# A recommender forward pass on one core: counts and sums 27 steps ahead of the token rows for 16, the last blocks of layers queued, five outputs of the last tile begun early, zero rows by transfer

## The chip, the cores and the metric

The kernel runs on one core of a Trainium2 chip. A core has TensorE (PE: matrix products, with a separate record, PEld, for its weight loads), VectorE (DVE), ScalarE (ACT), GpSimd (POOL) and SyncE (SP), and sixteen DMA engines which move data between HBM and the on-chip memory. Each engine works through its own instructions in the order of the program; semaphores make one wait for another. The metric is the device time in microseconds of one launch, as the median of several runs.

## The reference

For each of 16384 examples, 32 token ids pick rows of 300 numbers from a table of 50000 rows, and their mean is taken. Three fields of 20 ids each pick rows of 64 numbers from tables of 1000, 5000 and 10000 rows, and the mean is taken in each. Four single ids pick rows of 64 from tables of 100, 50, 20 and 1000 rows. The eight parts are joined to 748 numbers and go through three dense layers of 1024, 512 and 256 outputs. Beside this, every id of the seven small tables has one scalar ("wide"), and all of them are added to the last product.

```python
tok = word_emb[token_idx].mean(axis=1)              # 32 rows of 300
e1 = emb_mh1[mh1_idx].mean(axis=1)                  # 20 rows of 64; e2, e3 alike
...
o1 = emb_oh1[oh1_idx]                               # one row of 64; o2, o3, o4 alike
emb = jnp.concatenate([tok, e1, e2, e3, o1, o2, o3, o4], axis=1)
wide = (wide_mh1[mh1_idx].sum(axis=(1, 2)) + ... + wide_oh4[oh4_idx][:, 0])[:, None]
h = jax.nn.relu(emb @ W1 + b1)
h = jax.nn.relu(h @ W2 + b2)
h = jax.nn.relu(h @ W3 + b3)
return jax.nn.sigmoid(h @ Wd + bd + wide)
```

All of it is float32.

## The kernel before

**Tiles.** The examples are cut into 128 tiles of 128. Three things are done for each tile.

*Token rows.* POOL gathers the rows by indirect DMA: one DMA takes one token position of the 128 examples (L279). Two positions share a buffer `tok_rows` of a pool with `TOK_BUFS` buffers, so a tile has 16 groups of two gathers. DVE adds a group to the running sum `own` in PSUM (L260 for the first group of a tile, L262 and L267 for each later one); the last addition of a tile writes into the tile's feature buffer `g`. The additions stand `TOK_LAG` = 3 groups behind the gathers in the program. There are 2048 groups, and with the lag `n_all` = 2051 units of work. The gather of a group waits until the buffer it takes was added up.

*Small tables.* They are never gathered. An id is split into a high part (which slice of 128 rows of the joined tables, 138 slices in all) and a low part (which row in it). DVE writes one-hot rows of both parts (L344), ACT scales half of one (L351), PE multiplies them for each pair of examples (L362), which gives the counts of every table row, and ACT evicts these to `cnt` (L365). Then PE multiplies the counts with the tables, slice by slice, 138 products a tile (L397), and DVE evicts the sums to `g` (L387). There is one PSUM buffer `pg` for these sums. The tables are held as three bfloat16 terms per number (`terms`), which are made at the start from raw rows (`load_tables`, `convert_tables`, L168 to L223). Where a table's length is not a multiple of 128, the rows that are missing are set to zero by DVE (L180).

*Layers.* When all features of a tile are there, PE transposes `g` in six chunks (L435) and DVE evicts them, scaled, to `x` (L439). Tiles are joined to blocks of `LAYER_TILES` = 3; the last two tiles, 126 and 127, are blocks of their own. I number blocks by their place for the threes (block 41 holds tiles 123 to 125) and by their tile for the two single ones (block 126, block 127). `mlp` (L509) is the work of a block: three layers (L493, evicted by ACT at L504), the last product `po` (L524), the addition of the wide term on DVE (L529), the sigmoid on ACT (L530) and the transfer of the result by SP (L532). The outputs of layers 1, 2 and 3 lie in turn in two buffers, "odd" and "even"; the third shares its buffer with the first, and the result row that SP sends out lies in it too.

**The order.** It is written out by hand in one loop over steps (L607). A tile's counts take `STEPS` = 11 steps, t is the tile whose counts are made and i the step in it; the sums of tile t − 1 run in the same 11 steps, in portions given by i. The loop has `n_steps` = 128 x 11 + `WAKE` steps. Token work is spread evenly over all of them (`toks.to(n_all * (step + 1) / n_steps)`, L650), so counts and sums drift ahead of the token rows from 0 steps at the start to `WAKE` at the end, and the last `WAKE` steps hold token rows and layers but no counts.

A tile that has its sums and its wide term is put on the list `waiting`; at a later step, when its tokens are added up, its transposes are emitted (L637 to L642). When a block has all its tiles, the layers of the block before are finished at once, whatever is left of them, and the new block's are begun (L643 to L649). Layers are generators that yield after every product, wrapped in `Paced`: each step takes as many products as brings the block to its share of the steps up to a limit, `left` (L649), which is where the tokens of the next block are complete (`ready`) and no later than `EARLY` = 3 steps before the end.

Evictions are kept on lists so that they come behind other work of the same step: `later` for DVE's (emitted by `flush`), `pending` for ACT's. At step `n_steps` − 3, `early_part` begins four of the eight outputs of layer 1 of the last tile, with the three chunks that need no tokens. Behind the loop come what is left of the layers, the other three transposes of tile 127, and its layers.

Of the kernel before, what the change touches and what calls it, by code (L numbers as in the profile page):

```python
# [8 lines left out]
F32 = mybir.dt.float32  # L9
# [5 lines left out]
AF = mybir.ActivationFunctionType  # L15
# [3 lines left out]
P = 128  # L19
N_TOK, TOK_D = 32, 300  # L20
N_MH, EMB = 20, 64
ROW = EMB + 1
D1, D2, D3 = 1024, 512, 256
TOK_GROUP = 2
TOK_LAG = 3
TOK_BUFS = 7
HOT_BUFS = 3
WAKE = 16
EARLY = 3
BLOCK = 256  # L30
LAYER_TILES = 3
LAST_TILES = 2
# [9 lines left out]
LAYER_TIME = 2.5  # L42
# [20 lines left out]
def kernel(  # L63
# [29 lines left out]
    for f in SMALL:  # L93
        n = -(-tables[f].shape[0] // P)
# [2 lines left out]

    tokp = ctx.enter_context(tc.tile_pool(name="tok", bufs=TOK_BUFS))
    const = ctx.enter_context(tc.tile_pool(name="const", bufs=1))
    idxp = ctx.enter_context(tc.tile_pool(name="idx", bufs=3))  # L100
    keyp = ctx.enter_context(tc.tile_pool(name="keys", bufs=1))
    scp = ctx.enter_context(tc.tile_pool(name="sc", bufs=2))
    ohp = ctx.enter_context(tc.tile_pool(name="onehot", bufs=HOT_BUFS))
    cp = ctx.enter_context(tc.tile_pool(name="counts", bufs=2))
    gp = ctx.enter_context(tc.tile_pool(name="g", bufs=2))
    wp = ctx.enter_context(tc.tile_pool(name="wide", bufs=2))
    xp = ctx.enter_context(tc.tile_pool(name="x", bufs=2))
    hp = ctx.enter_context(tc.tile_pool(name="h", bufs=1))
# [2 lines left out]
    ps_g = ctx.enter_context(tc.tile_pool(name="ps_g", bufs=1, space=bass.MemoryType.PSUM))  # L111
# [45 lines left out]
    first = const.tile([P, 2, N_SMALL], I32, name="first")  # L157
# [7 lines left out]
    minus_count = const.tile([P, P], BF16, name="minus_count")  # L165
    nc.vector.tensor_single_scalar(minus_count, ident, -1.0 / COUNT, op=ALU.mult)

    def load_tables(part0, tag):  # L168
        raw = hp.tile([P, PART, ROW], F32, name="raw", tag=tag)
        for f in SMALL:  # L170
            table, (h0, h1) = tables[f], slices[f]
            full, rest = divmod(table.shape[0], P)
            a, b = max(h0, part0), min(h0 + full, part0 + PART)
            if a < b:
                nc.sync.dma_start(
                    out=raw[:, a - part0 : b - part0, :],
                    in_=table[(a - h0) * P : (b - h0) * P, :].rearrange("(h p) d -> p h d", p=P),
                )
            if rest and part0 <= h0 + full < part0 + PART:
                nc.vector.memset(raw[:, h0 + full - part0, :], 0.0)  # L180
                nc.sync.dma_start(out=raw[0:rest, h0 + full - part0, :], in_=table[full * P :, :])
        return raw

# [229 lines left out]
    class Block:  # L413
# [2 lines left out]

        def __init__(self, first, n):
            self.first, self.n, self.missing = first, n * P, NK * n
            self.x = xp.tile([P, NK, N], F32, name="x")

        def transpose(self, t, ks):

# [34 lines left out]
    def early_part(block):  # L457


        part = []  # L460
        for pair in range(2):
            two = ps_c.tile([P, 2, 512], F32, name="pc")
            for m in range(2):
                part.append(two[:, m, :])
                for k in range(N_EARLY):
                    nc.tensor.matmul(
                        part[-1][:, 0 : block.n],
                        w1_sb[: chunk_k[k], k, (2 * pair + m) * P : (2 * pair + m + 1) * P],
                        block.chunk(k),
                        start=(k == 0),  # L470
                        stop=False,
                    )
        return part

    pending = []

    def flush_outputs():
        while pending:
# [2 lines left out]
    def layer(dst, weights, bias, srcs, n_out, part=None):  # L481


        n = srcs[0].shape[-1]
        for m in range(n_out):
            begun = part is not None and m < 4
            ph = part[m] if begun else ps_h.tile([P, N], F32, name="ph", tag="ph")
            for k, src in enumerate(srcs):
                if begun and k < N_EARLY:
                    continue  # L490
                if k == len(srcs) - 1:
                    flush_outputs()
                nc.tensor.matmul(  # L493
                    ph[:, 0:n],
                    weights[: src.shape[0], k, m * P : (m + 1) * P],
                    src,
                    start=(k == 0),
                    stop=(k == len(srcs) - 1),
                )
                if k < len(srcs) - 1:  # L500
                    yield 1

            def evict(m=m, ph=ph):
                nc.scalar.activation(dst[:, m, 0:n], ph[:, 0:n], AF.Relu, bias=bias[:, m : m + 1])  # L504

            pending.append(evict)
            yield 1

    def mlp(block, part=None):  # L509


        n = block.n
        h1 = hp.tile([P, M1, N], F32, name="h1", tag="odd")
        yield from layer(h1, w1_sb, b1_sb, [block.chunk(k) for k in range(NK)], M1, part)
        h2 = hp.tile([P, M2, N], F32, name="h2", tag="even")
        yield from layer(h2, w2_sb, b2_sb, [h1[:, k, 0:n] for k in range(M1)], M2)
        flush_outputs()
        h3 = hp.tile([P, M3 + 1, N], F32, name="h3", tag="odd")
        yield from layer(h3, w3_sb, b3_sb, [h2[:, k, 0:n] for k in range(M2)], M3)
        po = ps_h.tile([1, N], F32, name="po", tag="ph")  # L520
        for k in range(M3):
            if k == M3 - 1:
                flush_outputs()
# [4 lines left out]
        y = h3[0:1, M3, 0:n]  # L528
        nc.vector.tensor_add(y, po[:, 0:n], block.wide())  # L529
        nc.scalar.activation(y, y, AF.Sigmoid, bias=bd_sb)  # L530
        b0 = block.first * P
        nc.sync.dma_start(out=out[b0 : b0 + n, :].rearrange("n o -> o n"), in_=y)  # L532

    class Paced:

# [50 lines left out]
    def ready(t):  # L586

        return max(-(-(n_groups * (t + 1) + TOK_LAG) * n_steps // n_all) + 1, (t + 2) * STEPS + 2)

    def block_for(t):  # L590
        if t not in block_of:
            n = ends[t] - t
            block = Block(t, n)
            block_of.update({t + k: block for k in range(n)})
        return block_of[t]
# [7 lines left out]
    sc, evict = key_columns(lookup_keys(ix))  # L603
    evict()
    hot = one_hots(sc, 0, 0)
    layers, cnt, sums, waiting = None, None, None, []
    for step in range(n_steps):  # L607
        t, i = divmod(step, STEPS)
        s = t % NSUB
# [24 lines left out]
            flush_outputs()  # L634
        if sums:
            run_sums(sums, early_sums.get(i, 0), step, step)
        if waiting and step >= waiting[0][0]:  # L637
            _, k, ks = waiting[0]
            if k in summed or ks[0] < N_EARLY and k == tiles - 1:
                waiting.pop(0)  # L640
                block = block_for(k)
                later.append((step, block.transpose(k, ks)))  # L642
                if not block.missing:  # L643
                    flush(step)
                    if layers:
                        layers.finish()
                    layers = Paced(mlp(block), LAYER_TIME * block.n / P)
                    last = block.first + block.n // P
                    begin, left = step, min(ready(ends[last] - 1) if last < tiles else n_steps, n_steps - EARLY) - step  # L649
        toks.to(n_all * (step + 1) / n_steps)  # L650
        if t < tiles and more and s == 1 and i == 5:
            next_sc, evict = key_columns(next_keys)
# [2 lines left out]
        if sums:  # L655
            ahead = n_h * (i + 1) / STEPS - sums_done[i + 1]
        if layers:
            layers.to(mlp_work * layers.size * (step + 1 - begin) / left + ahead)
        if sums:
            run_sums(sums, late_sums.get(i, 0), step, step + 1)  # L660
        flush(step)
        if i == 0 and 2 <= t <= tiles + 1:
            wide_term(features(t - 2))
            if t - 2 < tiles - 1:
                waiting.append((step + 2, t - 2, range(NK)))
            else:
# [48 lines left out]
```

## Time and profile before

| | |
|---|---|
| time, median of 3 runs | 5194.64 us (5194.57 to 5196.89) |
| the profiled execution's time | 5194.91 us |
| its span, first to last instruction | 5193.1 us |
| mean granted TensorE clock | 0.990 |
| busy share PE / DVE / ACT / POOL | 92% / 72% / 52% / 75% |
| gathers of token rows | 4096, 0.946 us each |
| steady stretch of 250 us (4450 to 4700): PE / DVE / ACT / POOL busy | 234.96 / 181.80 / 132.41 / 189.36 us |

The busy share is the time in which an engine had an instruction under way, over the span. For PE it says little about its peak, since products are pipelined. A group of the profile is all instructions of one line, engine and kind; behind the bar stand their busy time, the mean of one, and the idle time of the engine just before them with what ended most of it. In a timeline a line is one instruction or a run of equal ones, with its start, its length, and in brackets the idle time before it and what ended it. A wait with "issue" behind it is one for which the profile shows nothing that was waited for.

### The profile page before, as it was taken

The page shows a single profiled execution, that of the slowest core. Times are in us where ns is not written, and L with a number is a line of the kernel's source. Part 1 is how long each engine was busy: PE and PEld are TensorE (multiplying, and loading weights), DVE is VectorE, ACT ScalarE, POOL GpSimd, SP SyncE. Part 2 cuts the span into 40 slices and gives each one's busy share as a digit, 9 for nine tenths or more (in the row PEclk, how much of TensorE's full clock was granted, in tenths as well). Part 3 has the DMA queues.
Part 4 walks back from the last instruction along what each step waited for, and adds up shares of the span by engine and source line. Part 5 has one row for each costly group of instructions (what it writes and reads, how often), then busy time and mean ns, then how long its engine had stood idle before and what let it go on. Part 6 is the DMA issues. An engine that isn't in the chain of part 4 may idle for free.

```text
span 5193.1 us, 92066 instructions
## 1 busy us (share of the span) xinstructions
PE 4795.8 (92%) x34812; PEld 3528.0 (68%) x34812; DVE 3733.3 (72%) x6662; ACT 2720.9 (52%) x3538; POOL 3877.1 (75%) x4103
## 2 busy tenths in 40 slices
PE   7899999999999999999999999999999999999999
PEld 4666666666666766666676666666666766766677
DVE  6777777777777777777777777777777777777773
ACT  6555555555555555555555555555555555555552
POOL 6777777777777777777777777777777777777774
PEclk9899999999999999999999999999999999999999
DMA  7444444444444444444444444444444444444442
GB/s 193 125 126 125 125 126 125 125 126 125 125 126 125 126 125 125 125 125 125 126 125 126 125 125 126 125 125 126 125 126 126 124 126 125 125 125 124 126 124 71
DMA packets 253394, 651.83 MB, mean 126 GB/s; under 512 B 119547, under 2 KB 120103, under 8 KB 252947
## 3 DMA queue, kind: packets, MB, share of 16 engines
q0 software_dynamic: 196608, 629.41, 44.7%
q1 hardware_dynamic: 56339, 16.53, 1.4%
q8 instruction: 272, 4.46, 0.4%
q14 instruction: 175, 1.43, 0.1%
HBM read 645.59 MB, written 0.07 MB: 124 GB/s over the span
## 4 chain that ended last, share of the span: by engine, by line
PE 52%; DMA 16%; DVE 14%; issue 10%; POOL 6%; ACT 1%; DVEq 0%; POOLq 0%; ACTq 0%
PE ph L493 29%; PE pg L397 16%; DMA tok_rows<-in_word_emb_dram,it 16%; POOL tok_rows L279 6%; PE pc L362 5%; DVE hot L344 5%; DVE own L267 3%; DVE own L262 2%; DVE g L387 2%; PE po L524 1%; PE pc L435 1%; DVE x L439 1%; PE left L211 0%; ACT hot L351 0%; ACT cnt L365 0%
## 5 line engine op out<-in xcount | busy, mean ns | idle before, releaser
L279 POOL DMA_INDIRECT tok_rows<-in_word_emb_dram,it x4096 | 3876.2, 946 | 1283.3 <-issue 774.0
L351 ACT ACTIVATE hot<-hot 64x768 bf16<-64x768 bf16 (+1 forms) x1408 | 1155.4, 821 | 1630.4 <-DVE hot L344 1619.8
L397 PE MATMUL pg<-terms,cnt 128*128 128x195 bf16 x17664 | 1736.8, 248 | 291.9 <-DVE g L387 291.9
L397 PEld LDWEIGHTS <-cnt 128*128 128x128 fp8e3 x17664 | 1521.4, 98 | 50.5 <-issue 32.9
L493 PE MATMUL ph<-x,w_sb 128*128 128x384 f32 (+3 forms) x4176 | 1491.3, 490 | 56.7 <-DVE x L439 56.7
L344 DVE TENSOR_TENSOR hot<-own,sc 128x1656 bf16<-128x1656 bf16 (+1 forms) x1408 | 1393.7, 990 | 83.3 <-PE pc L362 2.1
L365 ACT ACTIVATE cnt<-pc 128x828 uint16<-128x828 f32 (+1 forms) x1408 | 1185.6, 842 | 501.3 <-PE pc L362 480.4
L493 PE MATMUL ph<-h,w_sb 128*128 128x384 f32 (+1 forms) x3520 | 1230.3, 486 | 0.5 <-ACT h L504 0.5
L267 DVE TENSOR_TENSOR own<-own,tok_rows 128x300 f32<-128x300 f32 x1792 | 857.1, 478 | 425.9 <-DMA tok_rows<-in_word_emb_dram,it 380.8
L493 PEld LDWEIGHTS ph<-x,w_sb 128*128 128x128 f32 (+1 forms) x4176 | 729.0, 192 | 579.1 <-issue 191.3
L262 DVE TENSOR_TENSOR own<-own,tok_rows 128x300 f32<-128x300 f32 x1920 | 917.4, 478 | 248.7 <-DMA tok_rows<-in_word_emb_dram,it 191.6
L362 PEld LDWEIGHTS <-hot 128*128 128x128 bf16 x8192 | 596.6, 98 | 517.4 <-issue 296.8
L493 PEld LDWEIGHTS ph<-h,w_sb 128*128 128x128 f32 x3520 | 618.8, 192 | 442.6 <-issue 150.8
L362 PE MATMUL pc<-hot 128*128 128x138 bf16 x8192 | 733.4, 225 | 28.5 <-ACT hot L351 25.7
L504 ACT ACTIVATE h<-ph,b_sb 128x384 f32<-128x384 f32 (+1 forms) x612 | 350.1, 572 | 255.4 <-PE ph L493 240.8
L387 DVE TENSOR_REDUCE g<-pg 128x130 f32<-128x390 f32 (+1 forms) x512 | 260.9, 510 | 295.2 <-PE pg L397 293.2
L439 DVE TENSOR_TENSOR x<-pc,scale 128x768 f32<-128x768 f32 x127 | 120.5, 949 | 70.9 <-PE pc L435 70.9
L260 DVE TENSOR_TENSOR own<-tok_rows 128x300 f32<-128x300 f32 x128 | 61.3, 479 | 83.3 <-DMA tok_rows<-in_word_emb_dram,it 81.0
L331 DVE COPY sc<-pc 128x512 bf16<-128x512 bf16 x64 | 44.1, 690 | 99.2 <-PE pc L327 99.2
L435 PE MATMUL pc<-ident,g 128*128 128x128 f32 x762 | 104.9, 274 | 0.4 <-ACT cnt L365 0.4
L529 DVE TENSOR_TENSOR h<-po,x 1x384 f32<-1x384 f32 (+1 forms) x44 | 23.4, 533 | 88.3 <-PE po L524 88.3
L267 DVE TENSOR_TENSOR g<-own,tok_rows 128x300 f32<-128x300 f32 x128 | 60.2, 470 | 35.6 <-DMA tok_rows<-in_word_emb_dram,it 32.6
(48 smaller groups left out, 456.6 us busy)
## 6 DMA issues: line engine op xcount, KB each, us to landing
tok_rows<-in_word_emb_dram,it POOLq DMA_INDIRECT x4096
ix<-in_idx_dram SPq DMA_DIRECT2D x128, 32.0 KB
w_sb<-in_W_dram SPq DMA_DIRECT2D x6, 512.0 KB
raw<-in_mh_dram SPq DMA_DIRECT2D x4, 682.5 KB
it<-in_idx_dram SPq DMA_DIRECT2D x64, 32.0 KB
w_sb<-in_W_dram SPq DMA_DIRECT2D x1, 2048.0 KB
out_dram<-h SPq DMA_DIRECT2D x42, 1.5 KB
raw<-in_mh_dram SPq DMA_DIRECT2D x2, 227.5 KB
```

The costliest lines, as they stand in the source:

```text
L262: nc.vector.tensor_add(tok_sum, tok_sum, a)
L267: nc.vector.tensor_add(to, tok_sum, b)
L279: nc.gpsimd.indirect_dma_start(out=rows[:, r * TOK_D : (r + 1) * TOK_D], out_offset=None, in_=word, in_offset=bass.IndirectOffsetOnAxis(ap ...
L344: nc.vector.tensor_tensor(hot[:, 0 : 2 * rows, :].rearrange("p i (n d) -> p i n d", d=2), iota.rearrange("p (n d) -> p n d", d=2).unsqueez ...
L351: nc.scalar.activation(upper, upper, AF.Copy, scale=UPPER)
L362: nc.tensor.matmul(pc[:, k // n, at : at + n_h], hot[:, 2 * k, 0:P], hot[:, 2 * k + 1, :], start=True, stop=True)
L365: nc.scalar.activation(cnt[:, :, b : b + rows].rearrange("l h (g k) -> l h g k", g=2), pc[:, :, 0 : n * n_h].rearrange("l g (k h) -> l h g ...
L387: nc.vector.tensor_reduce(field_columns(features(t), pair), pg[:, 0:n, :].rearrange("p f (c d) -> p f d c", c=3), AX.X, ALU.add,)
L397: nc.tensor.matmul(pg[:, j, :], by_slice[:, h, :], terms[:, h, :], start=(h == h0), stop=(h == h1 - 1))
L439: nc.vector.tensor_tensor(self.x[:, ks[0] : ks[-1] + 1, at : at + P].rearrange("p (a c) b -> p a c b", a=banks), pt, scale[:, ks[0] : ks[- ...
L493: nc.tensor.matmul(ph[:, 0:n], weights[: src.shape[0], k, m * P : (m + 1) * P], src, start=(k == 0), stop=(k == len(srcs) - 1),)
L504: nc.scalar.activation(dst[:, m, 0:n], ph[:, 0:n], AF.Relu, bias=bias[:, m : m + 1])
```

## The change

Six things are changed.

1. `WAKE` goes from 16 to 27. `n_steps` goes from 1424 to 1435. To hold what lies between the counts and the tokens for longer, index buffers go from three to four and feature buffers `g` from two to three; the row buffers `TOK_BUFS` go from seven to six.
2. A block that is complete goes on a list `complete`. It begins at once only if no layers are under way or it ends before tile 127; block 126 therefore waits until the layers of block 41 are done. A block's limit comes from `deadline`: six steps (`LAST_LAYERS`) before the end for block 41, the end itself for block 126, and as before for the others. Block 127 keeps its `x` in a buffer of the counts' pool.
3. When the layers of a block have made all their products, they are finished in that step.
4. The end of a block (addition of the wide term, sigmoid, transfer) becomes a function on a list `rows_out`, and is emitted at the end of the step after, or when the next layers begin.
5. `early_part` begins five outputs instead of four; the fifth lies in the PSUM buffer `pg` of the sums.
6. The missing rows of a table are set to zero by a DMA of SP from a zero buffer, instead of by DVE.

```diff
-TOK_BUFS = 7
+TOK_BUFS = 6
...
-WAKE = 16
+WAKE = 27
 EARLY = 3
+LAST_LAYERS = 6
...
-    idxp = ctx.enter_context(tc.tile_pool(name="idx", bufs=3))
+    idxp = ctx.enter_context(tc.tile_pool(name="idx", bufs=4))
...
-    gp = ctx.enter_context(tc.tile_pool(name="g", bufs=2))
+    gp = ctx.enter_context(tc.tile_pool(name="g", bufs=3))
...
+    zeros = const.tile([P, ROW], F32, name="zeros")
+    nc.vector.memset(zeros, 0.0)
...
-                nc.vector.memset(raw[:, h0 + full - part0, :], 0.0)
+                nc.sync.dma_start(out=raw[rest:P, h0 + full - part0, :], in_=zeros[rest:P, :])
                 nc.sync.dma_start(out=raw[0:rest, h0 + full - part0, :], in_=table[full * P :, :])
...
-            self.x = xp.tile([P, NK, N], F32, name="x")
+            if first + n < B // P:
+                self.x = xp.tile([P, NK, N], F32, name="x")
+            else:
+                self.x = cp.tile([P, NK, n * P], F32, name="x_last", tag="counts")
...
+        part.append(ps_g.tile([P, 2, 3 * ROW], F32, name="pg").rearrange("p f d -> p (f d)"))
+        for m, to in enumerate(part):
+            for k in range(N_EARLY):
+                nc.tensor.matmul(
+                    to[:, 0 : block.n],
...
-    pending = []
+    pending, rows_out = [], []
+
+    def flush_rows():
+        while rows_out:
+            rows_out.pop(0)()
...
-            begun = part is not None and m < 4
+            begun = part is not None and m < len(part)
...
         n = block.n
+        flush_rows()
         h1 = hp.tile([P, M1, N], F32, name="h1", tag="odd")
...
+        def finish():
+            y = h3[0:1, M3, 0:n]
+            nc.vector.tensor_add(y, po[:, 0:n], block.wide())
+            nc.scalar.activation(y, y, AF.Sigmoid, bias=bd_sb)
+            b0 = block.first * P
+            nc.sync.dma_start(out=out[b0 : b0 + n, :].rearrange("n o -> o n"), in_=y)
+
+        rows_out.append(finish)
...
+    def deadline(block):
+
+        last = block.first + block.n // P
+        ahead = tiles - 1 - last
+        if ahead == 1 and block.n > P:
+            return n_steps - LAST_LAYERS
+        return ready(ends[last] - 1) if ahead > 0 else n_steps
...
+        outputs = list(rows_out)
...
                 if not block.missing:
-                    flush(step)
-                    if layers:
-                        layers.finish()
-                    layers = Paced(mlp(block), LAYER_TIME * block.n / P)
-                    last = block.first + block.n // P
-                    begin, left = step, min(ready(ends[last] - 1) if last < tiles else n_steps, n_steps - EARLY) - step
+                    complete.append(block)
+        if complete and (layers is None or layers.done >= layers.total or complete[0].first + complete[0].n // P < tiles - 1):
+            flush(step)
+            block = complete.pop(0)
+            if layers:
+                layers.finish()
+            layers = Paced(mlp(block), LAYER_TIME * block.n / P)
+            layers.total = mlp_work * layers.size
+            begin, left = step, max(deadline(block) - step, 1)
...
-            layers.to(mlp_work * layers.size * (step + 1 - begin) / left + ahead)
+            layers.to(mlp_work * layers.size * min((step + 1 - begin) / left, 1) + ahead)
+            if layers.done >= layers.total:
+                layers.finish()
...
         flush(step)
+        if outputs and rows_out[: len(outputs)] == outputs:
+            flush_rows()
...
-    layers.finish()
+    while complete or layers:
+        layers.finish()
+        layers = Paced(mlp(complete.pop(0))) if complete else None
...
     Paced(mlp(block, part)).finish()
+    flush_rows()
```

More of the change, by code (lines that the diff above doesn't have):

```diff
@@ L462, in early_part @@
             two = ps_c.tile([P, 2, 512], F32, name="pc")
[L463 to L472, printed above, removed]
-        return part
-    pending = []
+            part += [two[:, 0, :], two[:, 1, :]]
+        part.append(ps_g.tile([P, 2, 3 * ROW], F32, name="pg").rearrange("p f d -> p (f d)"))
[3 more added lines that the diff above has]
+                    to[:, 0 : block.n],
+                    w1_sb[: chunk_k[k], k, m * P : (m + 1) * P],
+                    block.chunk(k),
+                    start=(k == 0),
+                    stop=False,
+                )
+        return part
+    pending, rows_out = [], []
+    def flush_rows():
+        while rows_out:
+            rows_out.pop(0)()
     def flush_outputs():
@@ L527, in mlp @@
             yield 1
[L528 to L532, printed above, removed]
+        def finish():
[5 more added lines that the diff above has]
+        rows_out.append(finish)
     class Paced:
@@ L605 @@
     hot = one_hots(sc, 0, 0)
-    layers, cnt, sums, waiting = None, None, None, []
+    layers, cnt, sums, waiting, complete = None, None, None, [], []
     for step in range(n_steps):
```

## The prediction

> **What bounds the kernel now.** I read the busy shares first, then the groups, then the gathers in order of time.
>
> ```profile
> PE 4795.8 (92%) x34812; PEld 3528.0 (68%) x34812; DVE 3733.3 (72%) x6662; ACT 2720.9 (52%) x3538; POOL 3877.1 (75%) x4103
> ...
> L279 POOL DMA_INDIRECT tok_rows<-in_word_emb_dram,it x4096 | 3876.2, 946 | 1283.3 <-issue 774.0
> ```
>
> The shares point at PE. They mislead: a gather is 0.946 us busy and is followed by 0.30 us in which POOL waits for nothing, so POOL at 75% is full. The timeline of POOL shows starts 1.25 us apart from end to end, with four holes:
>
> ```profile
> 59.41 0.95 POOL L279 DMA_INDIRECT tok_rows<-in_word_emb_dram,it  x1 [0.30 <-issue]
> 64.31 0.94 POOL L279 DMA_INDIRECT tok_rows<-in_word_emb_dram,it  x1 [3.95 <-DVE own L260]
> ...
> 84.05 0.94 POOL L279 DMA_INDIRECT tok_rows<-in_word_emb_dram,it  x1 [5.04 <-DVE own L267]
> ...
> 5110.89 0.94 POOL L279 DMA_INDIRECT tok_rows<-in_word_emb_dram,it  x1 [8.31 <-DVE own L267]
> ...
> 5141.28 0.94 POOL L279 DMA_INDIRECT tok_rows<-in_word_emb_dram,it  x1 [18.21 <-DVE own L267]
> ...
> 5160.04 0.94 POOL L279 DMA_INDIRECT tok_rows<-in_word_emb_dram,it  x1 [0.31 <-issue]
> ```
>
> 4095 intervals of 1.25 us are 5119 us. Above the usual 0.30 us the holes hold 3.65 + 4.74 us at the start and 8.01 + 17.91 us at the end. So the middle is bound by POOL, and the end by whatever makes DVE late. The timeline of DVE names it (number in brackets: idle before, and who ended it):
>
> ```profile
> 63.34 0.34 DVE L180 MEMSET raw<- 128x65 f32 x4 [3.38 <-PE left L211]
> ...
> 81.13 0.69 DVE L331 COPY sc<-pc 128x512 bf16<-128x512 bf16 x1 [8.71 <-PE pc L327]
> ...
> 5057.02 0.47 DVE L267 TENSOR_TENSOR g<-own,tok_rows 128x300 f32<-128x300 f32 x1 [0.40 <-DMA tok_rows<-in_word_emb_dram,it]
> ...
> 5109.16 0.56 DVE L387 TENSOR_REDUCE g<-pg 128x130 f32<-128x390 f32 x1 [15.31 <-PE pg L397]
> ...
> 5133.57 0.96 DVE L439 TENSOR_TENSOR x<-pc,scale 128x768 f32<-128x768 f32 x1 [19.37 <-PE pc L435]
> ```
>
> From 5057.5, when tile 125 is added up, DVE waits for PE, not for rows. PE runs almost without a gap from the transposes of that tile to the last product:
>
> ```profile
> 5061.25 0.81 PE L435 MATMUL pc<-ident,g 128*128 128x128 f32 x6
> ...
> 5064.84 3.50 PE L493 MATMUL ph<-x,w_sb 128*128 128x384 f32 x10
> ...
> 5169.30 0.49 PE L435 MATMUL pt<-ident,g 128*128 128x128 f32 x3
> ```
>
> So the end is 5061.25 + 131.87 us of PE work and output = 5193.12. That stretch is where the change can pay.
>
> **WAKE 27.** A step now carries 2051/1435 = 1.429 row groups (1.440 before) and lasts 3.575 us at POOL's pace (3.602). Tile 125 is complete in step 1412 (before: 1401), and counts end with step 1407 in both. Hence, from its transposes on, PE no longer meets:
> - 28 count products of L362: 4 x 0.36 + 0.24 = 1.7 us (the layer's next product starts 0.36 us after a row of six);
> - 138 of the 180 sums of L397 between 5064.84 and 5166.5: a row of 20 moves its follower by 1.73 us, so 0.0865 each, 11.9 us. The 42 of tile 127 in its columns 6 to 10 stay;
> - two waits of 0.66 us for DVE g L387: 1.3 us.
>
> Together 14.9 us. None of it vanishes: 11 steps of counts and sums go into the 5050 us before. What hides it is DVE waiting for rows: 380.8 + 191.6 + 81.0 + 32.6 = 686 us in the list of waits, 0.48 us per step, against 0.027 us by which a step gets shorter. PE is busy 232.8 of 250 us there, 3.354 us per step: 93.8% of the new step. Without that cover the 11 steps cost 11 x 3.6 = 40 us.
>
> **Six row buffers.** A gather of group m + 6 now waits for group m's addition. From the starts of gathers and the ends of additions I took the margin: with seven buffers the median is 12.3 us, and six take 2.5 us off. Between groups 100 and 2000 the smallest left is 2.4 us, so no new hole there. At the start it costs. The hole at 84.05 ends with the key columns of L331, after PE had worked without a gap from 62.2 to 84; with six buffers POOL stands there one group, two gathers, further back: **+2.5 us**. Bounds: +2.5, and 2.5 − 3.38 = −0.9 if PE should get those keys earlier. I take +2.5: tile 125 is complete at 5057.5 + 2.5 = 5060.0. [...] the row shows the 0.30 us after each gather with or without free buffers, so I charge the single group.
>
> **Zero rows by transfer.** Seven memsets leave DVE (waits of 7.03 and 3.38 us at L180); the addition behind the last goes at about 60 instead of 63.6, so the first hole shrinks, but the second ends at the same moment. Nothing gained. SP issues seven more transfers at about 0.4 us (three of L181 took 1.10), ahead of the weight loads, which it issues from 65.5 to 79; no layer starts before 176. Nothing lost.
>
> **Blocks queued, outputs a step later.** Block 126 no longer forces block 41 to finish; it gets 16 steps, 57 us, for its 58.9 us (74.6 us from 5064.84 to the last po at 5139.46, less 1.7, 11.9, 1.3 and 0.8 of transposes). PE's order hardly waits for rows, so the queueing moves waits off DVE rather than work off PE. What was late on DVE (L529 waited 88.3 us for po in 39 places) is mostly gone; behind it stood the additions. The output transfer leaves SP up to one step, 3.6 us, later; SP stood 3152.6 us at that line before, with index loads behind it, so they start no later than they did. The third g buffer, fourth index buffer and x_last keep 126 and 127 from waiting on 125; they add no instruction.
>
> The new adjacency: block 126 follows 41, and 127 follows 126, with nothing between, and the first eviction of a layer overwrites the buffer that the output transfer reads. In the old order it was issued at 5140.78 and the next eviction ran at 5142.90, so it landed within 2.1 us; its packet ended 0.78 us after issue. Addition 0.55, sigmoid 0.6, landing 1.1[...]: PE waits 0 to 0.4 us a time. [...] I take the row: **+0.4**; the wait of 0.46 us for ACT at 5163.7 goes in exchange. Bounds −0.5 and +2.5.
>
> **Five outputs early.** Six more products before the last rows, six fewer behind: 6 x 0.116 = 0.7 us. With PE bound it only changes place: 0.
>
> **The sum.** PE reaches tile 125's transposes about 0.5 us after 5060.0 (3.8 us late before, with counts and sums in front; bounds 0 and 3.8). 5060.5 + 131.9 − 14.9 + 0.4 − 0.5 = **5177.4 us span**. The profiled run took 5194.91, 1.8 more than its span, and stands 0.3 us over the median of 5194.64; so 5177.4 + 1.8 − 0.3 = **5179 us**, 15.6 less. The last rows are added up at 5139.9 (5160.04 − 25.92 + 2.5, and 3.4 from gather to sum), while PE comes to their transposes at 5154: the next thing late is still PE.
>
> **Rivals.**
> - Rows bound the end: PE does the tail in less than I count, or is never late, and the last tile waits for its rows at 5140; 23.1 us follow (23.8 from 5169.30 less 0.7): span 5163, **5165 us**. For: POOL is full elsewhere. Against: 14 us of PE work too much.
> - The six buffers leak in the middle: DVE, at some sums or blocks, is later than the margin, and 0.1 us lost per tile x 128 = 12.8 us gives **5192**. For: margins fall to 2.4–4 us after group 1700. Against: none reaches zero.
> - **Slower**: the 11 steps are not hidden. If a step cannot go below its 3.602 us because the chain of one-hot, counts, sums and evictions sets it, tile 125 completes 11 x 3.602 = 39.6 us later than 5057.5, at 5097, and 5097.6 + 116.9 gives a span of 5214.5, **5216 us**. It decides from 0.011 us per step (15.6 over 1413). For: PE is 93% busy. Against: DVE's 0.48 us.
> - That WAKE does nothing is excluded: it enters the step count.
>
> **Chances.** Forecast 0.66, rows bound 0.17, leak 0.09, slower 0.08. No change means within 0.2%, 10.4 us: 5184.3 to 5205. The forecast's own range is 5174 to 5187; about 0.03 of it lies above 5184. Faster 0.80, same 0.12, slower 0.08. The range reaches down to the second case and up to the forecast's end: 5166 to 5188.
>
> **What would show it.** POOL: holes of about 2 us at 60 and 8 us before 84, near 5110–5141 none over a few us. PE: transposes of tile 125 at 5060–5062 without counts after; po of block 41 near 5129; the last three transposes at 5154. If PE stands idle for over 3 us ahead of these, rows bound the end. Gathers with recurring holes, or starts of tile 125 after 5070, would make the forecast wrong.

## The result, and the profile after

| | before | after |
|---|---|---|
| median of 8 runs each | 5194.24 us (5192.52 to 5196.89) | 5178.8 us (5177.48 to 5181.08) |
| ratio to before | | 0.997, 95% interval 0.996 to 0.9981 |
| profiled execution, its span | 5194.91, 5193.1 us | 5177.48, 5175.7 us |

The kernel became 15.4 us faster by the medians. The profiled execution of the changed kernel is the fastest of its eight, so the two spans differ by more, 17.4 us.

The changed kernel has other line numbers: L279 became L283 (gather), L267 L271 (addition), L344 L348 (one-hots), L362 L366 (counts), L387 L391 (eviction of sums), L397 L401 (sums), L435 L442 (transposes), L439 L446, L493 L505 (layers), L524 L537 (po), L529 L544 (addition of the wide term). The busy shares and the group of gathers on its page:

```profile
PE 4786.2 (92%) x34812; PEld 3524.4 (68%) x34812; DVE 3732.3 (72%) x6656; ACT 2719.7 (53%) x3538; POOL 3875.7 (75%) x4103
...
L283 POOL DMA_INDIRECT tok_rows<-in_word_emb_dram,it x4096 | 3874.8, 946 | 1258.2 <-issue 788.3
```

Nothing to be seen there: the same instructions, six fewer on DVE (seven memsets out, one in), and shares within a point of those before. The idle time of POOL fell from 1283.3 to 1258.2, and that is the change. Its timeline has two holes left, and the last gather:

```profile
59.25 0.94 POOL L283 DMA_INDIRECT tok_rows<-in_word_emb_dram,it  x1 [1.53 <-DVE own L264]
82.55 0.94 POOL L283 DMA_INDIRECT tok_rows<-in_word_emb_dram,it  x1 [8.61 <-DVE own L271]
...
5133.60 0.95 POOL L283 DMA_INDIRECT tok_rows<-in_word_emb_dram,it  x1 [0.30 <-issue]
```

The holes of 8.0 and 17.9 us at the end are gone, and the last gather starts 26.4 us earlier. The kernel gained less than that, because the rows are not what the end waits for. DVE in the tail, and then PE:

```profile
5056.59 0.47 DVE L271 TENSOR_TENSOR g<-own,tok_rows 128x300 f32<-128x300 f32 x1 [0.81 <-DMA tok_rows<-in_word_emb_dram,it]
...
5110.36 0.96 DVE L446 TENSOR_TENSOR x<-pc,scale 128x768 f32<-128x768 f32 x1 [8.29 <-PE pc L442]
...
5137.95 0.47 DVE L271 TENSOR_TENSOR g<-own,tok_rows 128x300 f32<-128x300 f32 x1 [2.13 <-DMA tok_rows<-in_word_emb_dram,it]
5152.71 0.56 DVE L446 TENSOR_TENSOR x_last<-pt,scale 128x384 f32<-128x384 f32 x1 [14.29 <-PE pt L442]
```

```profile
5056.83 0.83 PE L442 MATMUL pc<-ident,g 128*128 128x128 f32 x6
...
5061.01 2.85 PE L505 MATMUL ph<-x,w_sb 128*128 128x384 f32 x8
...
5126.07 1.55 PE L537 MATMUL po<-h,wd_sb 128*1 128x384 f32 x4
...
5152.12 0.55 PE L442 MATMUL pt<-ident,g 128*128 128x128 f32 x3
```

The first and third rows of DVE are the last additions of tiles 125 and 127. DVE has the features of tile 127 at 5138.4 and then waits 14.3 us for PE, which comes to their transposes at 5152.1. So PE bounds the tail before and after. From the transposes of tile 125 to the end it took 131.87 us before and takes 5175.72 − 5056.83 = 118.9 us now: 13.0 of the 17.4 us. The other 4.4 is that it begins them at 5056.83 instead of 5061.25.

### The profile page after: what moved, and what is told of

It reads as the page before. It is cut to its first block, busy times and chain, and to the rows that moved or that the text cites. A ratio compares the mean times of both kernels' runs of the same rounds, so it can differ in the third digit from the quotient of the medians.

```text
span 5175.7 us, 92043 instructions
## 1 busy us (share of the span) xinstructions
PE 4786.2 (92%) x34812; PEld 3524.4 (68%) x34812; DVE 3732.3 (72%) x6656; ACT 2719.7 (53%) x3538; POOL 3875.7 (75%) x4103
## 3 DMA queue, kind: packets, MB, share of 16 engines
q14 instruction: 175, 1.43, 0.1%
## 4 chain that ended last, share of the span: by engine, by line
PE 49%; DMA 17%; DVE 15%; issue 11%; POOL 7%; ACT 0%; DVEq 0%; POOLq 0%; ACTq 0%
PE ph L505 27%; DMA tok_rows<-in_word_emb_dram,it 17%; PE pg L401 14%; POOL tok_rows L283 7%; DVE hot L348 5%; PE pc L366 5%; DVE own L271 4%; DVE own L266 3%; DVE g L391 2%; PE po L537 1%; PE pc L442 1%; DVE own L264 0%; DVE x L446 0%; ACT hot L355 0%; DVE ix L317 0%
## 5 line engine op out<-in xcount | busy, mean ns | idle before, releaser
L283 POOL DMA_INDIRECT tok_rows<-in_word_emb_dram,it x4096 | 3874.8, 946 | 1258.2 <-issue 788.3
L401 PE MATMUL pg<-terms,cnt 128*128 128x195 bf16 x17664 | 1734.8, 248 | 324.7 <-DVE g L391 324.7
L401 PEld LDWEIGHTS <-cnt 128*128 128x128 fp8e3 x17664 | 1519.2, 98 | 50.8 <-issue 32.4
L505 PE MATMUL ph<-x,w_sb 128*128 128x384 f32 (+2 forms) x4128 | 1476.8, 490 | 17.4 <-DVE x L446 17.1
L348 DVE TENSOR_TENSOR hot<-own,sc 128x1656 bf16<-128x1656 bf16 (+1 forms) x1408 | 1392.9, 989 | 83.3 <-PE pc L366 3.7
L505 PE MATMUL ph<-h,w_sb 128*128 128x384 f32 (+1 forms) x3520 | 1238.7, 488 | 0.0
L271 DVE TENSOR_TENSOR own<-own,tok_rows 128x300 f32<-128x300 f32 x1792 | 856.9, 478 | 400.8 <-DMA tok_rows<-in_word_emb_dram,it 354.3
L505 PEld LDWEIGHTS ph<-x,w_sb 128*128 128x128 f32 (+1 forms) x4128 | 718.6, 191 | 556.0 <-issue 203.9
L366 PEld LDWEIGHTS <-hot 128*128 128x128 bf16 x8192 | 597.5, 97 | 511.9 <-issue 285.6
L505 PEld LDWEIGHTS ph<-h,w_sb 128*128 128x128 f32 x3520 | 619.5, 193 | 434.3 <-issue 150.8
L366 PE MATMUL pc<-hot 128*128 128x138 bf16 x8192 | 731.8, 225 | 28.6 <-ACT hot L355 23.4
L391 DVE TENSOR_REDUCE g<-pg 128x130 f32<-128x390 f32 (+1 forms) x512 | 261.1, 510 | 324.1 <-PE pg L401 321.7
L446 DVE TENSOR_TENSOR x<-pc,scale 128x768 f32<-128x768 f32 x127 | 121.2, 954 | 107.3 <-PE pc L442 106.5
L442 PE MATMUL pc<-ident,g 128*128 128x128 f32 x762 | 106.4, 277 | 0.4 <-ACT cnt L369 0.4
L442 PEld LDWEIGHTS pc<-ident,g 128*128 128x128 f32 x762 | 84.5, 143 | 16.3 <-issue 7.7
L271 DVE TENSOR_TENSOR g<-own,tok_rows 128x300 f32<-128x300 f32 x128 | 60.2, 470 | 34.8 <-DMA tok_rows<-in_word_emb_dram,it 32.1
```

What stands on the lines that cost most here:

```text
L271: nc.vector.tensor_add(to, tok_sum, b)
L283: nc.gpsimd.indirect_dma_start(out=rows[:, r * TOK_D : (r + 1) * TOK_D], out_offset=None, in_=word, in_offset=bass.IndirectOffsetOnAxis(ap ...
L348: nc.vector.tensor_tensor(hot[:, 0 : 2 * rows, :].rearrange("p i (n d) -> p i n d", d=2), iota.rearrange("p (n d) -> p n d", d=2).unsqueez ...
L366: nc.tensor.matmul(pc[:, k // n, at : at + n_h], hot[:, 2 * k, 0:P], hot[:, 2 * k + 1, :], start=True, stop=True)
L391: nc.vector.tensor_reduce(field_columns(features(t), pair), pg[:, 0:n, :].rearrange("p f (c d) -> p f d c", c=3), AX.X, ALU.add,)
L401: nc.tensor.matmul(pg[:, j, :], by_slice[:, h, :], terms[:, h, :], start=(h == h0), stop=(h == h1 - 1))
```

## The experiments

Twelve kernels ran, in three groups, each group on one chip beside the kernel before. In the first group (the first four rows) every kernel is some 13 us slower (the kernel before 5207.33); the last section shows where that time goes. So a kernel is compared with the kernel before of its own group, and "against the changed kernel" means: less the 15.4 us by which that one stood under the kernel before. The intervals are some 7 to 16 us wide, so those of two kernels 5 us apart overlap: what such a difference comes from is read from the traces. A hole is an interval between two gathers that exceeds their median by more than 0.02 us, counted with the excess. Middle means 120 to 5050 us; the holes there sum to 3.4 us before and 2.2 us after.

| kernel | median | kernel before | difference | ratio, 95% interval |
|---|---|---|---|---|
| 16 steps | 5208.44 | 5207.33 | +1.1 | 1.0003 (0.9995 to 1.0012) |
| 27 steps alone | 5202.98 | 5207.33 | −4.4 | 0.9991 (0.9983 to 1.0) |
| memsets kept | 5192.13 | 5207.33 | −15.2 | 0.9971 (0.996 to 0.9982) |
| 33 steps | 5189.44 | 5207.33 | −17.9 | 0.9966 (0.9953 to 0.9978) |
| before, six buffers | 5197.31 | 5195.18 | +2.1 | 1.0005 (0.9996 to 1.0013) |
| 27 steps alone, filler | 5186.61 | 5195.18 | −8.6 | 0.9984 (0.9977 to 0.999) |
| no queue | 5179.83 | 5195.18 | −15.4 | 0.997 (0.9958 to 0.9982) |
| 30 steps | 5175.05 | 5195.18 | −20.1 | 0.9961 (0.9947 to 0.9975) |
| outputs at once | 5184.02 | 5194.28 | −10.3 | 0.9979 (0.997 to 0.9988) |
| five buffers | 5182.44 | 5194.28 | −11.8 | 0.9977 (0.9967 to 0.9987) |
| no layers of 126 | 5167.68 | 5194.28 | −26.6 | 0.9948 (0.9933 to 0.9964) |
| 30 steps, split | 5189.14 | 5194.28 | −5.1 | 0.999 (0.9984 to 0.9997) |

### 16 steps in the changed kernel

```diff
-WAKE = 27
+WAKE = 16
```

> The changed kernel with the counts and sums 16 steps ahead again, all else as changed. If the gain is PE work taken out of the stretch behind tile 125 (28 count products and the sums, about 15 us), it all comes back: PE is 3 to 4 us late at tile 125's transposes near 5060 and needs some 132 us from there, span 5191 to 5194, time 5193 to 5196. If queueing the blocks and moving the outputs (holes of POOL closed) is what paid, the time stays under 5184.

The whole gain is gone: +1.1 us on the kernel before. The times are those of the first group, 13 us higher, but the profiled execution happened to run at the quicker spacing of gathers and can be read directly:

```profile
5063.08 0.82 PE L442 MATMUL pc<-ident,g 128*128 128x128 f32 x6
...
5172.02 0.55 PE L442 MATMUL pt<-ident,g 128*128 128x128 f32 x3
```

These are the transposes of tile 125 and the last three of tile 127. The span is 5195.6, 132.5 us from the first of them. POOL's holes in the tail are 12.4 us, where the kernel before has 25.9. So half of the holes closed and nothing was won: PE sets this end. That counts and sums leave the tail is the gain.

### 27 steps without the rest, and then with a filler

To the kernel before, only this was done:

```diff
-TOK_BUFS = 7
+TOK_BUFS = 6
-WAKE = 16
+WAKE = 27
...
-idxp = ctx.enter_context(tc.tile_pool(name="idx", bufs=3))
+idxp = ctx.enter_context(tc.tile_pool(name="idx", bufs=4))
...
-gp = ctx.enter_context(tc.tile_pool(name="g", bufs=2))
+gp = ctx.enter_context(tc.tile_pool(name="g", bufs=3))
```

> The kernel before with 27 steps and the buffers that they need (six of rows, four of indices, three of features), without queued blocks, late outputs, five early outputs or zero rows by transfer. If PE bounds the tail: tile 125 complete near 5059, some 119 us behind it, span 5177 to 5180, time 5179 to 5182; POOL has holes again near the end, which cost nothing as long as the last rows are added before PE comes to them at about 5153. If the queueing is needed, those holes push the rows past that point and the time is over 5186.

The second case, where the prediction, which gave the other edits no gain, held the first: 4.4 us gained, not 15. Two things are missing. The first is at the end, in PE's timeline:

```profile
5167.14 2.94 PE L466 MATMUL pc<-x,w_sb 128*128 128x128 f32 x24
5172.35 0.88 PE L435 MATMUL pt<-ident,g 128*128 128x128 f32 x3 [2.27 <-DVE g L267]
5173.89 2.50 PE L493 MATMUL pc<-x,w_sb 109*128 109x128 f32 x10 [0.65 <-DVE x L439]
...
5180.87 8.01 PE L493 MATMUL ph<-x,w_sb 128*128 128x128 f32 x48
```

POOL has a hole of 15.9 us ahead of it (it ends at 5147.5), so the last rows come late and PE waits 2.27 us for them. Behind the wait the same products take longer: the ten 2.50 us for 1.38, the forty-eight 8.01 us for 5.52 in the kernel before. A table of stretches shows why (start and end, length, busy us of PE, PEld, DVE, ACT and POOL, then the granted clock, the DMA share and GB/s):

```profile
5160.00:5170.00 10.00, 9.85 (x85) 9.11 (x83) 3.61 (x8) 2.24 (x6) 7.59 (x8) 1.00 0.47 124
...
5175.00:5180.00 5.00, 4.32 (x19) 3.73 (x18) 0.00 (x0) 0.87 (x3) 0.00 (x0) 0.50 0.00 0
5180.00:5185.00 5.00, 4.71 (x22) 4.72 (x23) 0.00 (x0) 0.97 (x3) 0.00 (x0) 0.50 0.00 0
```

The granted clock is 0.50 from 5172.4 for 13.7 us. The stretch from the last transposes to the end takes 29.4 us, 23.8 before: 5.6 us for the clock, on top of 2.3 of waiting. The filler tests that. It stands behind the early outputs; nobody reads it, and nothing else changes:

```diff
+    fill = ps_g.tile([P, 2, 3 * ROW], F32, name="pg")
+    for _ in range(32):
+        nc.tensor.matmul(fill[:, 0, :], minus_count, terms[:, 0, :], start=True, stop=True)
     for _, k, ks in waiting:
```

> The 27 steps alone, and 32 small products that nobody reads between the early outputs and the last transposes, so that TensorE works while it waits for the last rows. If the slow stretch behind that wait (granted clock 0.5 for 13.7 us) came from TensorE standing idle for 2.3 us, the clock stays at 1.0 and the last layers take 5 to 6 us less: 4 to 6 us under the 27 steps alone. If it has another cause, the time stays or rises by up to 0.5 us.

4.2 us less than without the filler (−8.6 against −4.4), as expected if the idle stretch brought the clock down. The two ran in different groups and their intervals overlap; the trace shows it directly, with no stretch at 0.50 behind 5012 us:

```profile
5159.52 2.86 PE L674 MATMUL pg<-terms,minus_count 128*128 128x195 bf16 x32
5162.30 0.55 PE L435 MATMUL pt<-ident,g 128*128 128x128 f32 x3
5163.50 1.38 PE L493 MATMUL pc<-x,w_sb 109*128 109x128 f32 x10 [0.65 <-DVE x L439]
...
5167.77 5.52 PE L493 MATMUL ph<-x,w_sb 128*128 128x128 f32 x48
```

32 useless products, and the ten take 1.38 us again, the forty-eight 5.52. The second thing is in the middle: holes there sum to 7.3 us with 27 steps alone and to 8.7 with the filler, among them, with the filler, 1.6 us at 3390 and 2.4 at 3513 (without it, 2.1 at 3520). Which of the other edits closes them was the next question.

### The queue undone

```diff
-        if complete and (layers is None or layers.done >= layers.total or complete[0].first + complete[0].n // P < tiles - 1):
+        if complete:
```

> The changed kernel with block 126 begun as soon as it is complete, so that the layers of block 41 are finished at once, ahead of the additions of rows on DVE. If the queue is what keeps the last rows early, POOL has a hole of 10 us or more near 5130, TensorE waits for the last rows about 2 us, the clock falls to 0.5 behind it, and the time is 6 to 9 us over the changed kernel. If the other edits do that work (late outputs, five early outputs), it stays within 2 us.

The second case. The hole came and the loss did not: the time is that of the changed kernel. POOL, DVE and PE at the place (three timelines):

```profile
5130.44 0.94 POOL L283 DMA_INDIRECT tok_rows<-in_word_emb_dram,it  x1 [14.35 <-DVE own L271]
```

```profile
5153.52 0.47 DVE L271 TENSOR_TENSOR g<-own,tok_rows 128x300 f32<-128x300 f32 x1 [2.08 <-DMA tok_rows<-in_word_emb_dram,it]
```

```profile
5154.19 0.55 PE L442 MATMUL pt<-ident,g 128*128 128x128 f32 x3
```

The last addition ends at 5153.99 and PE arrives at 5154.19. The hole takes 14 us from the rows, and they had 13.7 us to spare. The queue buys margin here and no time. The 27 steps alone lacked a little more, counted from the transposes of tile 125: their last rows were added up 97.0 us after them and not 95.75, and PE was there 94.8 us after them and not 95.95, with four outputs begun early and not five, and without the wait of 0.68 us for ACT that this kernel has at the start of block 126.

### Outputs at once

```diff
-        rows_out.append(finish)
+        finish()
```

> The changed kernel with a block's end (addition, sigmoid, transfer) emitted at once instead of a step later. The 27 steps alone had holes of POOL in the middle (1.6 and 2.4 us near 3400 and 3515, and some 3 us in small ones) that the changed kernel does not have. If the late outputs closed them, they are back: 4 to 7 us over the changed kernel, with tail unchanged in length. If finishing the layers in their own step or something else closed them: within 1 us of the changed kernel, no holes after 100 us.

5.2 us over the changed kernel, and the holes of the middle are back, 8.5 us in all; the two largest, 1.6 and 2.4 us, are where they were with 27 steps and the filler. DVE in this kernel at one of them:

```profile
3386.00 0.96 DVE L446 TENSOR_TENSOR x<-pc,scale 128x768 f32<-128x768 f32 x1 [0.99 <-PE pc L442]
3391.35 0.55 DVE L544 TENSOR_TENSOR h<-po,x 1x384 f32<-1x384 f32 x1 [4.39 <-PE po L537]
3391.82 0.46 DVE L264 TENSOR_TENSOR own<-tok_rows 128x300 f32<-128x300 f32 x1
```

and in the changed kernel, where the addition of the wide term comes a step later:

```profile
3386.55 0.55 DVE L544 TENSOR_TENSOR h<-po,x 1x384 f32<-1x384 f32 x1 [0.83 <-PE po L537]
```

At a block's start DVE evicts x behind a wait for PE and then stands 4.39 us more for the last product of the block before; the additions of rows are behind it, and six buffers do not last. With the output a step later the second wait is 0.83 us. Over the whole run DVE waits for the last product 124.8 us in 43 places with the outputs at once, and 51.2 us in 18 places in the changed kernel.

### Memsets kept

```diff
-                nc.sync.dma_start(out=raw[rest:P, h0 + full - part0, :], in_=zeros[rest:P, :])
+                nc.vector.memset(raw[:, h0 + full - part0, :], 0.0)
```

> The changed kernel with the missing rows zeroed on DVE again. The key columns on DVE should come about 1.5 us later (81.1 instead of 79.6), tile 125 likewise: 5179 to 5181, at most 1.5 us more and hardly to be told from none. If the zero rows carry a part of the gain, 5 us or more.

−15.2 against −15.4: no difference that can be measured. (The absolute times are those of the first group.) The first hole grows to 6.29 us of waiting and the second shrinks to 5.01, because both end where PE lets DVE go; the key columns come at 81.03.

### Row buffers: six in the kernel before, five in the changed one

```diff
-TOK_BUFS = 7
+TOK_BUFS = 6
```

> The kernel before with six row buffers instead of seven and nothing else. If my term for the buffers is right, the hole before 84 us ends at the same time with one group fewer gathered, everything behind it comes 2.5 us later, and the middle shows no new holes: 2 to 3 us over the kernel before. If six buffers are too few in the middle, recurring holes and 10 us or more.

```diff
-TOK_BUFS = 6
+TOK_BUFS = 5
```

> The changed kernel with five row buffers instead of six. If each buffer costs one group at the start and the margins of the middle hold: 2.5 us at the start and, from the few margins that are under 2.5 us with six buffers, up to 2.5 us more; the holes of the tail are hidden by TensorE: 3 to 5 us over the changed kernel. If a buffer less makes a hole that recurs with every tile or block: 10 us or more.

+2.1 us and +3.6 us, both where expected. The holes of the start sum to 10.2 us with six in the kernel before (8.5 with seven), and to 13.0 with five in the changed one (9.8 with six); the middle stays at 2.6 and 2.1. It is the first of the two holes that grows, from 3.7 to 5.4 us and from 1.2 to 4.6; the second stays (4.7 and 8.3). The interval of the kernel before with six buffers includes 1, so it is the trace that shows the term and not the time; and one profile is no exact measure either, since the three kernels with 27 steps that differ from the changed one only behind the start have 9.7 to 11.0 us there. The median interval is 1.251 us with five, six and seven buffers, so the gap of 0.30 us behind each gather is not one that buffers close. Seven buffers in the changed kernel were not tried.

### How far it goes: 33 steps, 30 steps, 30 steps with a split block

```diff
-WAKE = 27
+WAKE = 33
```

> The changed kernel with 33 steps. If the tail is bound by PE and the middle still has cover, the 62 sums left behind tile 125's transposes and their two waits go too: 62 x 0.0865 + 1.3 = 6.7 us less, span 5169, time 5171 to 5173, with PE still some 7 us behind the last rows. If the cover is used up, POOL shows holes in the middle and the time is 5179 or more.

2.5 us gained on the changed kernel, not 6.7. The tail is the length it should be, 5187.70 − 5074.92 = 112.8 us. But PE is late to it (tile 125 was added up at 5071.4):

```profile
5064.39 0.32 PE L401 MATMUL pg<-terms,cnt 128*128 128x195 bf16 x1 [3.02 <-DVE g L391]
5064.50 6.98 PE L505 MATMUL ph<-h,w_sb 128*128 128x384 f32 x12
...
5074.92 0.82 PE L442 MATMUL pc<-ident,g 128*128 128x128 f32 x6
```

With no counts left, PE ran out of work, waited 3.02 us for a sum's eviction, and was granted 0.50 of its clock for 6.8 us: the twelve products took 6.98 us, where twelve take 4.04 with 30 steps.

```diff
-WAKE = 27
+WAKE = 30
```

> The changed kernel with 30 steps. With 33 steps the tail got shorter by the 6 us expected, but TensorE had so little to do in the ten steps before that it waited 3.0 us for a sum, the clock fell to 0.5 for 6.8 us and it came 3.5 us late to tile 125. With 30 steps some 59 of the 62 sums still leave the tail (5.1 us and one wait of 0.7). If that wait does not reappear: 5 to 6 us under the changed kernel, ratio to the kernel before near 0.9960. If it does: 2 to 3 us, as with 33.

4.7 us under the changed kernel, a little short of the 5 to 6 expected; PE waits 0.98 us for the same eviction, the clock stays up (the twelve products take 4.04 us), and the tail is 5173.25 − 5058.72 = 114.5 us. **This is the fastest full kernel of the study**, 20.1 us under the kernel before.

```diff
-WAKE = 27
+WAKE = 30
...
-    sizes = [LAYER_TILES] * ((tiles - LAST_TILES) // LAYER_TILES) + [1] * LAST_TILES
+    sizes = [LAYER_TILES] * ((tiles - LAST_TILES) // LAYER_TILES - 1) + [2] + [1] * (LAST_TILES + 1)
```

> 30 steps, and the last full block split: tiles 123 and 124 as a block of two, 125 as a block of its own. TensorE then has 38 us less to do behind tile 125 but comes up to 20 us late to it, so POOL gets holes. With 30 steps TensorE is 10 us behind the last rows, so if the holes stay small the end moves up to where the rows set it: up to 8 us under 30 steps alone. If the holes delay the rows by 10 us or TensorE waits and its clock falls: equal to or up to 8 us over 30 steps.

Worse than I thought possible, 15 us over 30 steps alone. PE comes to the transposes of tile 125 only at 5087.35, not 20 but 29 us later than with 30 steps alone (5058.72): the block of two has to be finished ahead of them. DVE waits with it, and POOL has six holes from 5029 to 5097, 20.7 us in all. Then PE waits twice: 3.55 us at 5124 for DVE, with the clock at 0.50 for 6.8 us, and 5.59 us for the last rows, with 0.50 for 13.7 us.

### The layers of block 126 left out

```diff
-            layers = Paced(mlp(block), LAYER_TIME * block.n / P)
+            layers = Paced(mlp(block) if block.first != tiles - 2 else iter(()), LAYER_TIME * block.n / P)
```

> The changed kernel with the layers of block 126 left out (its 128 results are not computed), which takes some 21 us of TensorE work out of the tail. If TensorE bounds the tail with no other limit near, 21 us less. If the last rows are the next limit, TensorE stands idle about 7 us for them: 13 to 14 us less where its clock holds, and 7 to 9 us less where the clock falls to 0.5 behind the idle stretch as it did with the 27 steps alone.

11.2 us less than the changed kernel, for 21 us of work: between my two cases. PE waits for the rows, and the granted clock falls to 0.50 for 13.7 us:

```profile
5130.71 0.83 PE L474 MATMUL pg<-x_last,w_sb 128*128 128x128 f32 x6
5137.55 0.90 PE L442 MATMUL pt<-ident,g 128*128 128x128 f32 x3 [6.01 <-DVE g L271]
5139.10 2.50 PE L505 MATMUL pc<-x_last,w_sb 109*128 109x128 f32 x10 [0.65 <-DVE x_last L446]
```

28.5 us follow, 23.6 in the changed kernel; so of the 9.8 us that are missing about 4.9 us is the clock, and the rest is waiting. This is the floor under the tail as long as the rows come at this pace: it is not the 5165 us that I gave for "rows bound the end" but some 3 us more, for which the 4.9 us of slow clock behind the wait are enough.

## Why the prediction was right, and where it was not

**The bound of the middle**: right. The intervals of the gathers have the same median before and after, 1.251 us, and the middle has holes of 3.4 and 2.2 us.

**WAKE 27, the main term**: right in kind, shown by the 16 steps, which lose the whole gain. Its size was 14.9 us for counts, sums and waits. One piece was mis-sized: I placed the transposes of tile 125 in step 1413 with 42 sums behind them; they are emitted in step 1412, and 62 sums follow, 1.7 us more. Six products of block 40 are left instead of four, 0.65 us. The tail has 118.9 us, not 116.9.

**Tile 125 complete at 5060.0**: it was at 5057.1. The two holes of the start sum to 9.8 us and not the 11.0 I reckoned, the first gather starts 0.2 us sooner, and the middle lost 1.2 us less. PE was there at once and not 0.5 us late. The +2.5 us for the buffer stands as a term, 2.1 us in the kernel before with six and 3.6 with five in the changed one, but not where I placed it: the first hole of the start grows, not the one before 84 us.

These errors, 3.7 us one way and 2.0 the other, leave the span at 5175.7 for 5177.4. The median, 5178.8 for 5179, is closer still by luck: I took the profiled run to stand 0.3 us over the median, and that of the changed kernel stands 1.3 us under it.

**Handing over between blocks**: 0.4 us; measured 0.23 us at block 126 and 0.81 for 0.51 us at block 127, 0.5 us in all. ACT, which has to wait for the output transfer there, goes on 1.43 and 1.19 us after its issue. The 1.1 us of landing was my estimate between the two figures of the kernel before, 0.78 us to the end of the packet and 2.1 us to the next eviction; ACT's two times stand 0.3 and 0.1 us above it.

**The outputs a step later**: here the prediction was wrong, although nothing of it shows in its sum. It gave the deferral no time, since "PE's order hardly waits for rows", and it took six buffers as safe from margins measured with 16 steps. The run with the outputs at once shows 5.2 us and 6.4 us more holes in the middle. The rival "the six buffers leak in the middle", which got 0.09, is what happens without this edit, at half the size it was given. The step that failed is the margin: read with 16 steps it was 2.4 us at the least, and the kernel before with six buffers does keep its middle (2.6 us of holes) although its outputs go at once. With 27 steps it did not carry over: between groups 100 and 2000 the smallest is 0.3 us with the outputs at once and 3.3 us in the changed kernel. Nor are the waits for po "mostly gone": of 88.3 us, 51.2 are left.

**The queue**: I gave it no time, and it has none. The 27 steps alone had made me doubt that, but of what they lack, the late outputs are shown to close the holes of the middle, and the queue alone does not make PE wait at the end. What share the five early outputs have there was not tried.

**The slower rival** (the 11 steps are not hidden): excluded. The 33 steps hide 17 more of them than the kernel before, with a middle that holds 2.8 us of holes.

**What I left out**: the clock. The rival "rows bound the end" took PE's time behind its wait as unchanged. Four traces of this study show a fall at the end, behind waits of 2.3 us (27 steps alone), 3.0 (33 steps), 3.6 and 5.6 (30 steps, split) and 6.0 us (no layers of 126), with 0.50 for 13.7, 6.8, 6.8, 13.7 and 13.7 us. The length of the wait alone does not give the price: 13.7 us stand behind the shortest and behind the longest.

## What to carry to other kernels

When one engine sets the pace of the middle and another the end, look for work that the second can do before the end at the first one's pace: the same instructions, moved by a step count, were worth 15 us here, and a further three steps 5 more. Ask of each order on an in-order engine what stands behind an instruction that waits; an output that nobody needs soon should not stand in front of the additions that free a buffer. And do not let TensorE run dry ahead of the last stage: here the products behind waits of 2.3 to 6.0 us at the end ran at a granted clock of 0.50 and took longer than the same products without one (ten took 2.50 us for 1.38), so a little backlog is better than none.

## What the runs showed of the hardware that was not expected

- **A short wait, a long price.** TensorE idle for 2.27 us brought the granted clock to 0.50 for 13.7 us and cost 5.6 us; 32 products without use took the loss away. A wait of 6.0 us cost about as much (4.9 us).
- **A longer wait without a fall, and falls in the middle.** In the middle of the kernel before and of the changed one the granted clock is 0.50 for 3.41 us in 17 places each. The last of them in the changed kernel, with as long a stretch ahead of it (columns as in the table of stretches above):

```profile
4996.61:5000.02 3.41, 1.30 (x10) 0.75 (x9) 1.90 (x4) 1.23 (x2) 2.50 (x4) 1.00 0.46 124
5000.02:5003.43 3.41, 3.37 (x7) 1.85 (x7) 2.83 (x5) 0.84 (x1) 2.66 (x3) 0.50 0.50 134
```

  PE was busy for 1.30 us of the 3.41 us ahead of this fall. With the 27 steps alone it was busy for 1.14 of the 3.41 us ahead of the fall at the end. A wait of 2.50 us, ended at 5037.95 in the kernel before, brought no fall, although it is longer than the 2.27 us at that end: the clock is 1.00 from 5030 to 5045, and PE was busy for 2.09 and 2.24 us of the two stretches of such length that the wait lies across (5033.36 to 5036.77 and on to 5040.19). What decides between a fall and none was not shown, nor what the falls cost in the middle.
- **Two spacings of gathers.** Between holes, a gather follows the last by 1.2501 us in most profiles and by 1.2531 in three of the four of the first group. Over 4095 intervals that is 12.3 us, which fits the 13 us by which that group is slower; the kernel before has no profile in it. The run with 16 steps had one execution of 5197.36, its profiled one with the short spacing, and eleven of 5207 to 5211. What switches it was not found.
- **The spacing of gathers did not change with DVE's work.** In the kernel before they follow each other by 1.25 us from 5114.63 to 5122.13, where DVE waits for PE, and by 1.24 to 1.25 from 5110.89 to 5114.63, where it adds row after row.
